# Four-layer graph kernel, layer 1: two adjacency gathers asked earlier, feature scaling one tile ahead instead of two, and SyncE's last adjacency tile ahead of a read-back

## The chip, the cores and the metric

One core of a Trainium2 chip runs the whole program. The metric is the device time of one execution in microseconds (us); the median of three executions stands for a kernel. Beside the times there is one profiled execution, with a trace of every instruction and every DMA packet.

## The reference

Four layers act on a graph of N = 2708 nodes with D = 128 features. `adj` (2708 x 2708, float32) is sparse, a fraction of a per cent of its entries, and has a filled diagonal. After each layer the input is added and the rows are normalised:

```python
x = _layernorm(x + L0(x, adj, adj, W0, a0))   # signed attention, dense product with adj
x = _layernorm(x + L1(x, adj, W1, b1))
x = _layernorm(x + L2(x, adj, W2, a2))        # four-head attention over the neighbours
x = _layernorm(x + L3(x, adj, ...))           # a gelu message for each neighbour, a gelu update, a layernorm

def L1(H, A, W, b):
    A_t = A + eye(n)
    D_inv = A_t.sum(axis=1) ** -0.5
    HW = H @ W.T + b
    return relu(D_inv[:, None] * A_t * D_inv[None, :] @ HW)
```

Layer 1 therefore needs the row sums of `adj` before it can scale the rows of HW by D_inv. The kernel takes these sums from lists of each row's nonzero entries, which it builds with a search, and which layers 2 and 3 use as well.

## The kernel before

**Tiles.** Rows are handled in NB = 22 blocks of 128. A product of a layer with `adj` runs on TensorE (PE) in two passes, each over a share of the output columns. In layer 0 pass 0 covers columns 0 to 1535, pass 1 the rest; in layer 1 pass 0 covers 0 to 2047 (four PSUM banks), pass 1 the remaining 660 (one bank of 512 and one of 148). Each pass goes over all 22 row blocks `n`; block `n` needs one adjacency tile `ah` and one block of features. Every product of a block with one bank shows as two matmuls in the trace.

**Adjacency tiles.** All 88 tiles (2 layers x 2 passes x 22) go through one pool of 7 buffers. `load_ahead(limit)` (line 846) asks for further tiles in this order, up to the limit and at most 7 beyond the tiles whose products have been written into the program (`done`). Layer 0 and layer 1's pass 1 fetch plain blocks with DMAs of SyncE (line 860; 330 KB for a tile of layer 1's pass 1). Layer 1's pass 0 works on rows in an order sorted by degree (`PERM`), so its tiles of 1 MB are indirect gathers, issued by GpSimd (POOL, line 853). In numbers of the pool, tiles 0 to 43 are layer 0's, 44 to 65 layer 1's pass 0, 66 to 87 its pass 1.

**Order.** `pinned` (line 265) chains the compute instructions and the GpSimd gathers of each engine in the order in which the program writes them. SyncE's plain loads are not pinned; the scheduler places them by their dependencies. Each engine executes its own list in order, and an instruction that waits holds everything behind it.

**Layer 0, pass 1.** `each0` (line 979) runs once per block: it takes signs on ScalarE (ACT), searches rows on VectorE (DVE) and, for the last blocks, prepares layer 1. `features(k)` (945) is a GpSimd gather of block k of the table TH, which the `finish` steps of layer 0 write to DRAM, into HS. It is called for k = 0 at n = 18, for k = 1 at n = 19, and for k = 2 and 3 at n = 21. `given(range(8))` (935) at n = 21 turns the search results of blocks 0 to 7 into DS, the factor D_inv in sorted order: one VectorE sum and three GpSimd operations.

**The search.** `entries` (614) goes over the blocks: it gathers a block's rows whole (`nat`, 1.4 MB, GpSimd line 621, four buffers), finds the largest entries with VectorE's MAX8 and their places with FIND_INDEX8 (about 3 us each). It runs through layer 0's passes and layer 1's pass 0. `given_back(b)` (595) writes block b's list to the DRAM table TL, in the natural order of rows; GpSimd issues it.

**Layer 1, pass 0.** `each1` (1053) at block n, after the products of block n: at n = 1 a small product and copy that adjust W2 (L1065, L1066), `features(n + 4)`, a stretch of search (at 1.35 units), `given` for the next two blocks at each even n, and `weights(n + 2)` (952), which scales HS block n + 2 in place by DS on ScalarE. Blocks 0 and 1 are scaled ahead of the pass by `scale_first` (955). After `each1` come `load_ahead(base + n + 6)` and two steps of each unfinished `finish` generator of layer 0. `finish` (748) takes a bank of results through a fixed sequence: transposes on PE, sums on VectorE (L769), means on GpSimd (L306, L307), squares on ScalarE (L312), roots on GpSimd (L316 to L318), normalisation on ScalarE (L322), transposes (L787), a copy `xt` (L790), a product with W1 (L824), an addition on VectorE (L827) and the write of TH. Three such banks are still open when layer 1 begins, so their steps lie between the products of blocks 0 to 4.

**Layer 1, pass 1.** `each1` with h = 1 calls `given_back(9 + n)` up to the last block at n = 12. At n = 13 (`NB - GIVEN`) it calls `natural_lists` (1018): SyncE reads TL back into LN when all the writes of TL have landed, and GpSimd copies three further columns. At n = 19 `off_diagonals` (1034) makes TOPJ on VectorE from LN (L1043 to L1048). In this pass the products of blocks 18 to 21 are done last, bank by bank: bank 4 of the four blocks, then bank 5, with their results copied out (L922) and put through `finish`, which writes TA to DRAM. Pass 0 ends with the products of block 21 alone, and between its banks with the step that brings D_inv back into the order of rows (L577).

**After it.** Layer 2 begins with 22 GpSimd gathers `ga` (L1183) of TA by TOPJ; layer 3 with gathers `G` (L1449) of the table TD, which layer 2 writes.

Of the kernel before, what the change touches and what calls it, by code (L numbers as in the profile page):

```python
# [118 lines left out]
def sparse_path(  # L119
# [28 lines left out]
    nc = tc.nc  # L148
    N, D = x.shape
    NB = -(-N // P)  # L150
# [114 lines left out]
    def pinned(i):  # L265

        e = i.ins.engine
        if e in newest:
            tc.add_manual_dep(
                i.ins, newest[e].name,  # L270
                mybir.DependencyInfo(mybir.DependencyClass.NoSync, mybir.DependencyReason.DATA),
                reason="order",
            )
        newest[e] = i.ins
        return i
# [102 lines left out]
    with (  # L378
# [16 lines left out]
        def features(bs):  # L395
            n = len(bs)
            g = slice(bs[0], bs[-1] + 1)
            xt = transposed([X[:, b, :] for b in bs], ps)
            t = ps.tile([P, 4, D], F32, name="hw_ps")
            for i, b in enumerate(bs):  # L400
                nc.tensor.matmul(t[:, i, :], xt[:, blk(i)], W0, start=True, stop=True)
            nc.scalar.copy(H[:, g, :], t[:, :n, :])
            for i, b in enumerate(bs):
                junk = sb.tile([P, D], F32, name="junk")
                nc.vector.scalar_tensor_tensor(
                    junk, t[:, i, :], 1.0, A1, ALU.mult, ALU.mult, accum_out=U[:, b : b + 1]
                )
            parts(UW[:, g, :], U[:, g], sb, n)
# [176 lines left out]
    GIVEN = 9  # L585
# [131 lines left out]
    with (  # L717
# [119 lines left out]

        loaded, done = [], [0]  # L840

        def span_of(layer, h):
            half = PASSES[layer][h]
# [2 lines left out]
        def load_ahead(limit=4 * NB):  # L846
            while len(loaded) < min(limit, 4 * NB, done[0] + BUFFERS):
                (layer, h), jb = divmod(len(loaded) // NB, 2), len(loaded) % NB
                lo, hi = span_of(layer, h)
                a = incoming.tile([P, EDGE], F32, name="ah")[:, : hi - lo]  # L850
                loaded.append(a)
                if layer and not h:
                    pinned(G_.indirect_dma_start(
                        a, None, adjL, bass.IndirectOffsetOnAxis(ap=PERM[:, jb : jb + 1], axis=0)
                    ))
                    continue
                for side, at in ((adjL, 0), (adjR, EDGE)):
                    k = slice(max(lo, at), min(hi, at + side.shape[1]))
                    if k.start < k.stop:
                        nc.sync.dma_start(  # L860
                            a[:, k.start - lo : k.stop - lo],
                            side[blk(jb), k.start - at : k.stop - at],
                        )
# [71 lines left out]
        def given(bs):  # L935

            while summed[0] <= bs[-1]:
                search(0.5)
            g = slice(bs[0], bs[-1] + 1)
            pinned(V_.tensor_reduce(SD[:, g], V[:, g, :], AX.X, ALU.add))  # L940
            pinned(G_.tensor_tensor(SD[:, g], SD[:, g], SELF[:, g], ALU.add))
            pinned(G_.tensor_scalar(SD[:, g], SD[:, g], 1.0, 1e-30, ALU.add, ALU.max))
            pinned(G_.tensor_tensor(DS[:, g], SD[:, g], HALF[:, : len(bs)], ALU.pow))
# [8 lines left out]
        def weights(k):  # L952
            pinned(S_.activation(HS[:, k, :], HS[:, k, :], AF.Copy, scale=DS[:, k : k + 1]))  # L953
# [11 lines left out]
        for h, half in enumerate(PASSES[0]):  # L965
            blocks = range(half[0] * 4, min(NB, half[-1] * 4 + 4))
            z = pz.tile([P, BANK], F32, name="z")[:, :48].rearrange("p (b k) -> p b k", k=4)
            behind = []

            def pattern(z=z, blocks=blocks, behind=behind):  # L970

                n, m = behind.pop()
                for i in range(len(blocks)):
                    pinned(T_.matmul(
                        z[:, i, :], m[:, blk(i)], F4[:, n, :],
                        start=n == 0 and i == 0, stop=n == NB - 1, skip_group_check=True,
                    ))

            def each0(n, a, lo, hi, h=h, behind=behind, pattern=pattern):
                if h == 0 and n + 2 < NB:  # L980
                    scaled(n + 2)
                m = signs[n % 2]
                if h and n < 2:
                    nc.gpsimd.memset(m[:, hi - lo :], 0.0)
                pinned(S_.activation(m[:, : hi - lo], a, AF.Sign))  # L985
                if behind:
                    pattern()
                behind.append((n, m))
                if h == 0 and n in (0, 3):
                    next(ordered, None)  # L990
                if h == 0 and n == 3:
                    next(passes)
                if h or n >= 8:
                    search(0.75 if h else 1.0)
                if h and NB - 4 <= n < NB - 2:
                    features(n - NB + 4)
                if h and n == NB - 1:
                    given(range(EARLY))
                    features(2)
                    features(3)  # L1000

            if h == 0:
                ordered = order(pt, nat)
                next(ordered)

            def end0(z=z, blocks=blocks, pattern=pattern):
                pattern()
                g = slice(blocks[0], blocks[-1] + 1)
                sums = RZ[:, g]
                nb = len(blocks)  # L1010
                pinned(S_.copy(zc[:, :nb, :], z[:, :nb, :]))
                pinned(V_.tensor_copy(CNT[:, g], zc[:, :nb, 3]))
                pinned(V_.tensor_reduce(sums, zc[:, :nb, 0:3], AX.X, ALU.add))
                pinned(V_.tensor_scalar(sums, sums, 1e-30, None, ALU.max))
                pinned(V_.reciprocal(sums, sums))

            later = half_of(0, h, H, each0, end0, later)
        def natural_lists():

            i = nc.sync.dma_start(  # L1020
                LN[:, :, : 2 * SLOTS], TL.rearrange("(b p) c -> p b c", p=P)
            )
            for name in back:
                tc.add_manual_dep(
                    i.ins, name,
                    mybir.DependencyInfo(mybir.DependencyClass.Sync, mybir.DependencyReason.DATA),
                    reason="all rows are in their places",
                )
            pinned(i)
            pinned(G_.tensor_copy(LN[:, :, K_ - 3], DEG))  # L1030
            pinned(G_.tensor_copy(LN[:, :, K_ - 2], DG))
            pinned(G_.tensor_copy(LN[:, :, K_ - 1], part["part"].to_broadcast([P, NB])))
# [18 lines left out]
        for h in range(2):  # L1051

            def each1(n, a, lo, hi, h=h):
                if h:
                    if GIVEN + n < NB:
                        given_back(GIVEN + n)
                    if n == NB - GIVEN:
                        natural_lists()
                    if n == 19:
                        off_diagonals()  # L1060
                    next(placed, None)
                    return
                if n == 1:
                    t = pt.tile([P, BANK], F32, name="q_ps")[:, : D + 2 * HEADS]
                    pinned(T_.matmul(t, C, W2, start=True, stop=True))  # L1065
                    pinned(S_.copy(W2, t))  # L1066
                if n + 4 < NB:
                    features(n + 4)
                search(1.35)
                k = n + 4  # L1070
                if EARLY <= k < NB and k % 2 == 0:
                    given(range(k, k + 2))
                if n + 2 < NB:
                    weights(n + 2)

            def end1():
                if later_half:
                    return
                for _ in passes:
                    pass  # L1080
                in_order_of_rows(pt, dinv, DS)
                for g in (slice(0, NB // 2), slice(NB // 2, NB)):
                    pinned(V_.tensor_tensor(
                        H2[:, g, :], H2[:, g, :],
                        dinv[:, g].unsqueeze(2).to_broadcast([P, NB // 2, D]), ALU.mult,
                    ))

            later_half = h
            later = half_of(1, h, H2 if h else HS, each1, end1, later)
# [83 lines left out]
    with (  # L1173
# [146 lines left out]
        last = len(sets) - 1  # L1320
# [11 lines left out]
        for t in ROWS:  # L1332
            n = NG - WHOLE
# [40 lines left out]
    with (  # L1374
# [256 lines left out]
        for n, k in enumerate(ORDER):  # L1631
# [7 lines left out]
            if n + 1 < NB:  # L1639
# [3 lines left out]
                i, j = place[k]  # L1643
# [542 lines left out]
```

## Time and profile before

| | |
|---|---|
| median of 3 runs | 650.23 us |
| lowest, highest run | 648.41, 655.59 us |
| profiled execution | 651.11 us, span of its instructions 649.3 us |
| busy share of the span | PE 73%, DVE 70%, POOL 57%, ACT 34% |
| mean granted clock of TensorE | 0.819 |
| data moved | 124.29 MB, mean 191 GB/s |
| layer 1, pass 0: first product to start of pass 1 | 176.5 to 280.4 us |
| layer 1, pass 1: to the last product's successor | 280.4 to 319.0 us |

Times inside the execution are counted from the first instruction of the span. "Idle before" is the time in which an engine did nothing ahead of an instruction, and the name behind it is what ended that wait. A gather's or load's landing is the time at which its completion was seen. Busy time is an average over stages with different limits, so the stage around an edit is read by itself: by the rows of each engine in order of time and by windows of a few microseconds.

### The profile page before, as it was taken

The page shows a single profiled execution, that of the slowest core. Times are in us where ns is not written, and L with a number is a line of the kernel's source. Part 1 is how long each engine was busy: PE and PEld are TensorE (multiplying, and loading weights), DVE is VectorE, ACT ScalarE, POOL GpSimd, SP SyncE. Part 2 cuts the span into 40 slices and gives each one's busy share as a digit, 9 for nine tenths or more (in the row PEclk, how much of TensorE's full clock was granted, in tenths as well). Part 3 has the DMA queues.
Part 4 walks back from the last instruction along what each step waited for, and adds up shares of the span by engine and source line. Part 5 has one row for each costly group of instructions (what it writes and reads, how often), then busy time and mean ns, then how long its engine had stood idle before and what let it go on. Part 6 is the DMA issues. An engine that isn't in the chain of part 4 may idle for free. (4 is left out here: it accounts for less than half of the span.)

```text
span 649.3 us, 8661 instructions
## 1 busy us (share of the span) xinstructions
PE 476.5 (73%) x2795; PEld 330.4 (51%) x2795; DVE 454.7 (70%) x1299; ACT 220.3 (34%) x519; POOL 372.8 (57%) x473
## 2 busy tenths in 40 slices
PE   6779999997856999899687565764765754665561
PEld 5644444664423443366386564553655643654560
DVE  3756999999995999462346838548638774584964
ACT  3125656685214000149543662221211211212120
POOL 6102023243474677537167657777777777777771
PEclk9559999999877999999855555987866869668687
DMA  9988999999599999957322121111212111121210
GB/s 305 380 318 311 406 424 405 395 344 393 195 379 362 334 411 417 362 180 212 97 73 49 52 77 48 45 48 44 63 44 63 46 50 47 45 59 48 56 43 26
DMA packets 46886, 124.29 MB, mean 191 GB/s; under 512 B 10303, under 2 KB 25077, under 8 KB 40559
## 3 DMA queue, kind: packets, MB, share of 16 engines
q0 software_dynamic: 15200, 69.06, 29.7%
q1 hardware_dynamic: 25230, 51.28, 22.1%
q10 hardware_dynamic: 6400, 3.30, 1.9%
q8 instruction: 24, 0.39, 0.2%
q14 instruction: 32, 0.25, 0.1%
HBM read 118.55 MB, written 6.30 MB: 192 GB/s over the span
## 5 line engine op out<-in xcount | busy, mean ns | idle before, releaser
L1449 POOL DMA_INDIRECT G<-TD,LP x126 | 131.3, 1042 | 44.8 <-issue 32.9
L878 PE MATMUL acc<-ah,XD 128*128 128x512 f32 (+1 forms) x264 | 114.1, 571 | 1.0 <-ACT XD L746 1.0
L1539 PE MATMUL af_ps<-W,M 128*128 128x128 f32 x426 | 77.3, 350 | 37.7 <-ACT M L1529 36.3
L655 DVE FIND_INDEX8 VI<-VI,nat 128x8 uint32<-128x2707 f32 x34 | 100.8, 2972 | 0.0
L1539 PEld LDWEIGHTS af_ps<-W,M 128*128 128x128 f32 x426 | 72.0, 260 | 41.2 <-ACT M L1529 39.6
L1449 POOL DMA_INDIRECT G<-TD,LM x63 | 63.6, 1010 | 19.2 <-issue 18.9
L985 ACT ACTIVATE sign<-ah 128x1536 bf16<-128x1536 f32 (+1 forms) x44 | 58.1, 1328 | 44.6 <-issue 26.3
L878 PE MATMUL acc<-ah,HS 128*128 128x512 f32 x132 | 64.7, 628 | 11.4 <-DMA ah<-in_adjL,PERM 6.7
L878 PEld LDWEIGHTS acc<-ah,XD 128*128 128x128 f32 x264 | 48.1, 197 | 44.8 <-issue 42.3
L1529 ACT ACTIVATE M<-M 128x1152 f32<-128x1152 f32 (+1 forms) x21 | 23.7, 1128 | 98.5 <-DVE M L1524 97.1
L1477 PE MATMUL q_ps<-S,JOIN 128*128 128x128 f32 x130 | 26.4, 354 | 35.5 <-DVE S L1473 35.5
L621 POOL DMA_INDIRECT nat<-in_adjo,PERM x22 | 21.9, 994 | 46.6 <-issue 19.8
L878 PEld LDWEIGHTS acc<-ah,HS 128*128 128x128 f32 x132 | 25.8, 202 | 42.5 <-issue 35.8
L1473 DVE TENSOR_TENSOR S<-sd_ps,MB 128x256 f32<-128x256 f32 x22 | 9.3, 421 | 51.4 <-PE sd_ps L1471 51.4
L1477 PEld LDWEIGHTS q_ps<-S,JOIN 128*128 128x128 f32 x130 | 21.2, 242 | 44.9 <-DVE S L1473 44.9
L642 DVE MAX8 cand<-nat 128x8 f32<-128x338 f32 (+3 forms) x96 | 34.8, 436 | 2.7 <-DMA nat<-in_adjo,PERM 2.7
L635 DVE MAX8 VI<-nat 128x8 f32<-128x2707 f32 x12 | 35.6, 2966 | 0.0
L1489 DVE TENSOR_SCALAR W<-TAB,LL 128x128 f32<-128x128 f32 x126 | 34.1, 358 | 0.0
L878 PE MATMUL acc<-ah,H 128*128 128x512 f32 (+1 forms) x88 | 28.3, 466 | 2.9 <-DMA ah<-in_adjR 2.9
L953 ACT ACTIVATE HS<-HS,DS 128x128 f32<-128x128 f32 x22 | 8.8, 400 | 62.8 <-DMA HS<-TH,PERMB 40.0
L1549 ACT COPY aT<-af_ps 128x128 f32<-128x128 f32 x22 | 5.8, 265 | 69.6 <-PE af_ps L1539 69.6
L1183 POOL DMA_INDIRECT ga<-TA,TOPJ x22 | 23.4, 1065 | 9.8 <-issue 9.8
(333 smaller groups left out, 951.7 us busy)
## 6 DMA issues: line engine op xcount, KB each, us to landing
ah<-in_adjL SPq DMA_DIRECT2D x22, 768.0 KB, 14.0
ah<-in_adjR SPq DMA_DIRECT2D x44, 330.0 KB, 7.3
TOP<-in_high SPq DMA_DIRECT2D x5, 1408.0 KB
ah<-in_adjL SPq DMA_DIRECT2D x22, 256.0 KB, 7.7
G<-TD,LP POOLq DMA_INDIRECT x126, 2.5
TA<-XD ACTq DMA_DIRECT2D x5, 264.0 KB, 3.6
TH<-H ACTq DMA_DIRECT2D x5, 256.0 KB
TD<-YD SPq DMA_DIRECT2D x3, 384.0 KB, 2.8
```

What stands on the lines that cost most here:

```text
L621: pinned(nc.gpsimd.indirect_dma_start(t, None, adjo, bass.IndirectOffsetOnAxis(ap=PERM[:, b : b + 1], axis=0)))
L635: pinned(nc.vector.max(V[:, b, 0:8], t))
L642: pinned(nc.vector.max(c[:, 8 * k : 8 * k + 8], t[:, at]))
L655: pinned(nc.vector.max_index(IX[:, b, s], V[:, b, s], t))
L878: pinned(T_.matmul(acc[i][:, :w], weights[:, n, :], a[:, i * BANK : i * BANK + w], start=n == 0, stop=n == NB - 1,))
L985: pinned(S_.activation(m[:, : hi - lo], a, AF.Sign))
L1183: pinned(G_.indirect_dma_start(ga[:, i, :], None, TA, bass.IndirectOffsetOnAxis(ap=TOPJ[:, b : b + 1], axis=0)))
L1449: i = G_.indirect_dma_start(G[:, s, :], None, TD, bass.IndirectOffsetOnAxis(ap=source(k, s), axis=0), **bound,)
L1477: pinned(T_.matmul(q[:, i, :], JOIN[:, j, :], S[:, :D], start=True, stop=True))
L1489: pinned(V_.tensor_scalar(W[:, s, :], part["lane"], to, v, ALU.is_equal, ALU.mult))
L1529: pinned(S_.activation(M[:, :n, :], M[:, :n, :], AF.Gelu))
L1539: i = T_.matmul(to, a, b, start=start, stop=stop, skip_group_check=True)
```

## The change

Six edits, none of which adds or takes away an operation. Two of them only serve the third part.

```diff
-        loaded, done = [], [0]
+        loaded, done, asked = [], [0], [None]
...
-                        nc.sync.dma_start(
+                        asked[0] = nc.sync.dma_start(
...
-                if h and NB - 4 <= n < NB - 2:
-                    features(n - NB + 4)
+                if h and n == NB - 4:
+                    features(0)
                 if h and n == NB - 1:
+                    load_ahead(2 * NB + 2)
                     given(range(EARLY))
+                    load_ahead(2 * NB + 3)
+                    features(1)
                     features(2)
                     features(3)
...
+            tc.add_manual_dep(
+                i.ins, asked[0].ins.name,
+                mybir.DependencyInfo(mybir.DependencyClass.NoSync, mybir.DependencyReason.DATA),
+                reason="the last tile is asked for first",
+            )
             pinned(i)
...
-                    if n == NB - GIVEN:
+                    if n == 17:
                         natural_lists()
...
-                if n + 2 < NB:
-                    weights(n + 2)
+                if 2 <= n + 1 < NB:
+                    weights(n + 1)
```

- **Early gathers.** At the end of layer 0's pass 1 (n = 21) the gathers of pool tiles 45 and 46 (blocks 1 and 2 of layer 1's pass 0) are written into GpSimd's list, one ahead of `given(range(8))` and one behind it. Before, they came with the products of layer 0's last bank, after `features(3)`. `features(1)` moves from n = 19 to behind them. Tile 44 was and is asked after n = 17.
- **Scaling.** `weights` for blocks 2 to 21 is called one block later, at n = k - 1 instead of n = k - 2.
- **SyncE.** `natural_lists` is called at n = 17, when the program has written all 88 loads, and its read-back of TL gets an order dependency (no wait of its own) on the last of them: SyncE must request the last tile of pass 1 before the read-back.

## Prediction

> **What bounds the kernel now.** I began with the chain of waits, because it says which stretch sets the end, and then walked back from its start. Merged by line it names GpSimd's gathers of layers 2 and 3, and its first piece stands at 323 us:
>
> ```profile
> POOL 23%; issue 11%; DMA 6%; DVE 5%; PE 3%; ACT 1%; POOLq 0%; DVEq 0%; ACTq 0%
> ```
>
> ```profile
> 323.24 0.78 ACT squares L312 x4
> ...
> 331.44 1.20 POOL ga L1183
> ```
>
> From 331.44 on (start and length in us) GpSimd issues 22 gathers `ga` and then the `G` gathers nearly without a break, to the end. Nothing there is edited. Those gathers need table TA, which the end of layer 1 writes. So whatever layer 1 saves before 323 moves the whole rest by the same amount, and what it loses too. Next I read layer 1's two passes on TensorE (start, length, what, idle before and its releaser):
>
> ```profile
> 176.46 2.84 PE L878 MATMUL acc<-ah,HS 128*128 128x512 f32 x6 [0.67 <-ACT HS L953]
> ...
> 187.10 5.46 PE L878 MATMUL acc<-ah,HS 128*128 128x512 f32 x6 [6.73 <-DMA ah<-in_adjL,PERM]
> ...
> 204.42 2.08 PE L824 MATMUL q_ps<-W,xt 128*128 128x128 f32 x8 [4.79 <-ACT xt L790]
> ...
> 262.37 2.84 PE L878 MATMUL acc<-ah,HS 128*128 128x512 f32 x6 [3.20 <-ACT HS L953]
> ...
> 315.33 3.81 PE L878 MATMUL acc<-ah,H 128*128 128x512 f32 x10 [2.91 <-DMA ah<-in_adjR]
> ```
>
> One tile of the gathered pass takes 3.43 us where nothing waits (216.75, 220.19, 223.62 and so on), 22 of them 75.5 us; from 176.46 to the pass's end at 280.4 there are 104. The missing 28 us lie mostly before tile 4 (212.88): tile 1 waits for its adjacency, tile 3 stands behind a wait for `xt`. What holds `xt` is in ScalarE's and VectorE's rows:
>
> ```profile
> 203.49 0.40 ACT L953 ACTIVATE HS<-HS,DS 128x128 f32<-128x128 f32 x1 [6.14 <-DMA HS<-TH,PERM]
> 203.80 0.56 ACT L790 COPY xt<-o_ps 128x512 f32<-128x512 f32 x1
> ```
>
> ```profile
> 206.53 0.69 DVE L827 TENSOR_TENSOR H<-q_ps,B 128x512 f32<-128x512 f32 x1 [7.78 <-PE q_ps L824]
> ```
>
> ScalarE stands in order: the scaling of tile 4's features, asked two tiles ahead, waits until 203.47 for a gather issued at 189.67, and the copy behind it, the two products behind that and VectorE's row search wait too. From 207 to 264.4 VectorE then searches almost without a gap, and its last result (DS) releases the last tile's gathers (266.09 and 267.47). So the 7.78 us come back at the pass's end. Last, the windows (stretch, length, busy times of PE, PEld, DVE, ACT, POOL, PE clock, DMA share, GB/s):
>
> ```profile
> 171.00:174.00 3.00, 3.00 (x12) 1.56 (x11) 2.94 (x13) 0.02 (x1) 2.50 (x5) 1.00 0.67 181
> 174.00:177.00 3.00, 2.16 (x14) 1.48 (x13) 2.83 (x13) 1.18 (x4) 2.50 (x3) 1.00 0.73 307
> 177.00:180.00 3.00, 3.00 (x9) 1.28 (x8) 3.00 (x11) 1.19 (x5) 2.27 (x5) 1.00 0.48 98
> 180.00:183.00 3.00, 0.38 (x3) 0.14 (x1) 3.00 (x11) 1.24 (x7) 2.16 (x3) 1.00 0.85 332
> ```
>
> The transfers rest for 0.99 + 0.81 + 1.56 + 0.45 = 3.8 us here, while six tiles are still unasked; from 183 to 207 the share is 0.97 to 1.05.
>
> **Part 1, gathers of tiles 1 and 2.** Nothing is added: GpSimd issues the same instructions in another order, so its own time (0.95 + 0.30 us per issue) stays. The place is behind features(0), which waits for TH until 169.16, so the hole from 165 to 169 stays open. From the rows of before the new order is: features(0) 169.16, `nat` 170.47, tile 1 at 171.7 (it was 180.23), the sums to 175.05, tile 2 at 175.2 (was 181.54), features(1), (2), (3) at 176.7, 177.9, 179.2 (were 171.73, 175.24, 176.65), `nat` 180.5 (was 177.96), then as before; from 185 on nothing on GpSimd has moved. features(1) now stands behind 2 MB. `nat` alone landed at 176.76; 1 MB behind another took 2.5 us (landings 191.95, 194.43). Tile 1 lands near 179.3, tile 2 near 181.8, features(1) just behind (it landed 0.2 us behind `nat` before). Its scaling (0.40) ends near 182.5, so tile 1 starts at 182.5 instead of 187.10. The moved `nat` lands near 186 instead of 184.43; VectorE needs it only after 201, so that costs nothing. Next comes a catch: before tile 2 TensorE has transposes (L787) of a block that ScalarE normalises (L322) after GpSimd's L318, at 192.18 and not moved. They began at 194.71 and can begin at 192.9. TensorE therefore idles from 186.3 to 192.9, and its clock falls as it did after 6.73 us (0.50 in the windows from 186 to 192). Tile 2 then runs some 2 us longer and ends near 199.5, where it ended before. So by itself this part brings almost nothing until tile 3.
>
> **Part 2, scaling one tile ahead.** 20 of the 22 scalings move one step later in ScalarE's order; none is added. At step 2 the scaling is now tile 3's, whose features land near 182, not tile 4's. `xt` is copied near 196 instead of 203.80; L824 runs when tile 2 ends (199.5 instead of 204.42), VectorE's L827 at about 200.6 instead of 206.53: 5.9 us. The second block's norm needs its L318 (198.87; up to 1 us earlier, as its squares are) and ends near 199.5, so tile 3 starts near 201.5 instead of 207.14: 5.6 us. TensorE has no idle of 4.79 us before it, so the slow clock from 204 to 210 (0.50, 0.58) goes as well, worth about 1.2 us more. What is late next: the transfers. From 213 to 273 they are full but for 0.2 us at 222 and 0.5 at 225, and `nat` lands 0.1 us ahead of its search (252.24 for 252.33). They can move by the holes that close: of 3.8 us about 2 (1.8 remain before tile 1 is moving and around 182), 0.9 at 210 to 213, 0.7 at 222 to 228: 3.6; counted by landings instead (1 MB at 215.10, 5.25 us behind the one before, could follow in 2.5) 2 + 2.7 + 0.7 = 5.4. Search, transfers and TensorE thus allow 5.9, 3.6 to 5.4 and 5.6 to 6.8. The least decides; I take 5.0 for the end of the pass, nearer to the count by landings, since a row shows each of those, with 3.6 and 5.9 as ends.
>
> **Part 3, SyncE's last tile.** SyncE held the read-back LN<-TL at the head from 302.2 until TL had landed (308.42), and with it the request for tile 21, whose buffer TensorE left at 304.65 (tile 14):
>
> ```profile
> 308.61 0.38 SPq L1020 DMA_DIRECT2D LN<-TL  x1
> 309.10 2.47 SPq L860 DMA_DIRECT2D ah<-in_adjR  x1
> ```
>
> Asked at 304.8, landing 3.6 us later (the median of these loads), it is there at 308.4, well before TensorE wants it at 312.42. The 2.91 us of idle go. The ten products behind it took 3.64 us at a clock of 0.56; at full clock, two 512-wide ones of 0.43 us and eight 148-wide ones of 0.13 (the tile at 303.54, two of each, took 1.11) would take 1.9. So TensorE's L755 moves from 318.97 to between 316.1 and 314.3. The read-back is asked at 308.6 as before (its request waits on TL, not on the tile) and takes 4.94 us at the most; VectorE's four instructions behind it end at 315.71 or up to 1.3 earlier. L761 was at 319.61, so 315.0 to 315.7 is possible: 3.9 to 4.6 us; 2.9 if the clock is no better. I take 4.0. The three copies of LN's columns that move with it on GpSimd (0.23 each) have 13.86 us of idle behind them. The Trainium skill, "TensorE: Matmul & The Clock Gate", section "Why this matters for your kernels", advises against TensorE idle gaps above about 3 us, after which the clock halves. A gap of 2.91 us is below that, so by the rule this part would keep its 2.9 us alone and the whole would be 642.3. The trace doesn't agree in either direction: 2.91 us before 315.33 was followed by 0.56, 3.20 us before 262.37 by 1.00.
>
> **Sum.** 5.0 + 4.0 = 9.0 us. The profiled execution took 651.11 (span 649.3 and 1.8 around it), giving 642.1; it lies 0.9 above the median of 650.23, so on that scale 641.2.
>
> **The rivals.** *Transfers alone bound the pass*, or the search starves on a later `nat`: then closing the first hole is undone by the full stretch from 213 to 273, and pass 0 ends 0 to 2 us earlier; only part 3 is left, 644.2 to 646.2. For it speak the share near 1.0 and the 0.1 us margin; against it the holes after 207, which come from the same stall. The Trainium skill, "DMA: Bandwidth & Descriptors", section "Issuing engines are not separate DMA queues", says that all issuers share the same 16 engines, so that an earlier request wins only idle time; the full shares agree. *Part 3 is refilled*: the read-back, not the tile, is late, or TL comes later, and VectorE's search for TOPJ ends last: only pass 0's 5.0 us count, 645.2. Against it: TOPJ is 3.9 us early now. *The early gathers don't go early*, should GpSimd's order leave them behind the features: then `xt` is still free, but the 2 us of the first hole stay open: 5.0 - 2 + 4.0 = 7.0, so 643.2. Against it: their buffers were last read before 164. *Slower:* a scaling one tile ahead is too late. TensorE then waits before each tile for ScalarE as it did at 255.47, for 0.78 us; 20 times that is 15.6, less the 9.0: 656.8. It decides from the point where the scaling leaves ScalarE less than 0.8 us before the product; the features of tiles 14 and 16 landed only 1.4 and 0.5 us ahead. Against it: from step 5 on ScalarE does nothing but scalings in this pass, so the order has no other work to put ahead, and each starts when its features land.
>
> **How the numbers follow.** Forecast case 0.58; transfers bound 0.18; part 3 refilled 0.10; gathers not early 0.06; slower 0.08. Under 1% (6.5 us, so 643.7) a measurement of this kernel can't be told from no change. The forecast case falls short of that with some 0.04, where its low ends meet; of the three middle cases, 0.34 together, 0.08 go below it: faster 0.62, same 0.30, slower 0.08. The range runs from 637.9 (5.9 and 4.6 saved, and 1.8 for the distance of the lowest run shown from the median) to 647.0 (the worst of the middle cases, 646.2, with 0.8); outside it lie the slower case and about a tenth of the rest.
>
> **What would show it.** Right: `ah` gathers at about 171.7 and 175.2; tile 1 at 182 to 183; no wait of 6 us for HS before `xt`; L824 near 200; the search's last instruction 3.6 to 5.9 us before 264.4; LN<-TL as SyncE's last request of the layer, TensorE without the idle of 2.91; the first `ga` near 322. Wrong: the pass ending after 278, many waits of ScalarE's HS at TensorE, or VectorE's L761 right behind L1048 with `ga` later than 326.

## The result, and the profile after

The changed kernel takes 642.57 us, the median of four runs (640.0 to 647.11), beside 650.82 us for the kernel before in the same runs (median of four): a ratio of 0.986, 95% interval 0.982 to 0.991, or 5.9 to 11.9 us less. The forecast was 641.2 us. The profiled execution is the longest of the four, 647.11 us with a span of 645.3, so single numbers from it are read by stage. Here and below, ratios, their intervals and differences of means leave out runs more than 1.5% above the fastest of their kernel, a slower state; medians are of all runs. In the changed kernel VectorE's instructions behind the read-back are L1051 to L1056 (L1043 to L1048 before), the first `ga` is L1191, the read-back L1023.

TensorE in order of time (start, length, what, count, idle before and its releaser); the columns are the same in all such lists below:

```profile
184.24 4.54 PE L878 MATMUL acc<-ah,HS 128*128 128x512 f32 x6 [3.71 <-ACT HS L953]
...
193.92 1.63 PE L787 MATMUL o_ps<-TAB,XD 128*128 128x128 f32 x4 [4.05 <-ACT XD L322]
...
257.08 4.24 PE L878 MATMUL acc<-ah,HS 128*128 128x512 f32 x6 [3.04 <-ACT HS L953]
...
314.27 1.32 PE L787 MATMUL o_ps<-TAB,XD 128*128 128x128 f32 x4 [2.91 <-DVE XD L769]
```

Tile 1 starts 2.9 us earlier than before, tile 2's transposes (L787) 0.8 us earlier. The wait of 4.79 us before L824 is gone, as this list from 199 us on shows:

```profile
200.35 1.05 PE L824 MATMUL q_ps<-W,xt 128*128 128x128 f32 x8
201.24 0.60 PE L787 MATMUL o_ps<-TAB,XD 128*128 128x128 f32 x4
201.68 2.74 PE L878 MATMUL acc<-ah,HS 128*128 128x512 f32 x6
```

ScalarE copies `xt` 7 us earlier (203.80 before), straight behind tile 3's scaling, with no wait:

```profile
196.47 0.39 ACT L953 ACTIVATE HS<-HS,DS 128x128 f32<-128x128 f32 x1
196.76 0.56 ACT L790 COPY xt<-o_ps 128x512 f32<-128x512 f32 x1
```

The windows that held the hole in the transfers (stretch, length, busy times of PE, PEld, DVE, ACT, POOL, PE clock, DMA share, GB/s):

```profile
171.00:174.00 3.00, 3.00 (x12) 1.52 (x11) 2.93 (x12) 0.00 (x0) 2.48 (x5) 1.00 0.43 83
174.00:177.00 3.00, 2.15 (x14) 1.61 (x13) 2.93 (x14) 1.17 (x3) 2.68 (x3) 1.00 0.93 385
177.00:180.00 3.00, 3.00 (x8) 1.28 (x7) 2.90 (x15) 0.00 (x0) 2.28 (x3) 1.00 1.00 411
180.00:183.00 3.00, 0.52 (x3) 0.14 (x1) 3.00 (x8) 0.00 (x0) 2.54 (x5) 1.00 0.88 358
```

From 174 to 180 the DMA engines rest for 0.2 us instead of 2.4, but from 171 to 174 for 1.7 instead of 1.0; over the four windows it is 2.3 us instead of 3.8. From 204 to 260 the transfers are as good as full. At the end of layer 1 SyncE asks for the read-back last, and VectorE is what the end then waits for. First SyncE, then VectorE:

```profile
290.00 11.43 SPq L860 DMA_DIRECT2D ah<-in_adjR  x7
305.77 0.38 SPq L1023 DMA_DIRECT2D LN<-TL  x1
```

```profile
311.08 0.43 DVE L1051 CAST LN<-LN 128x528 f32<-128x528 uint32 x1 [13.39 <-DMA LN<-TL]
311.55 0.71 DVE L1052 TENSOR_TENSOR nat<-LN,ROW 128x528 f32<-128x528 f32 x1
312.29 0.71 DVE L1055 TENSOR_TENSOR LN<-LN,nat 128x528 f32<-128x528 f32 x1
313.04 0.18 DVE L1056 CAST TOPJ<-LN 128x22 uint32<-128x22 f32 x1
313.13 0.87 DVE L761 SCALAR_TENSOR_TENSOR y<-H,o_ps 128x128 f32<-128x128 f32 x4
```

TensorE runs through its last tile without idle and has L755 out at 310.38, but L761 stands in VectorE's order behind four instructions that wait for the read-back until 311.08.

Four stamps say where the time went. P0 is from the first product of layer 1's first pass to the first of its second pass, P1 from there to the first L761 behind the last products (the row with x4), G from the first product to the first `ga`.

| kernel | P0 | P1 | G |
|---|---|---|---|
| before | 103.96 | 39.19 | 154.98 |
| changed | 99.93 | 36.60 | 148.71 |
| changed, two more profiles | 99.80, 99.44 | 35.22, 35.38 | 147.38, 147.66 |

So against this one profile of the kernel before, pass 0 gives 4.0 to 4.5 us, pass 1 2.6 to 4.0, and layer 1 as a whole up to the first `ga` 6.3 to 7.6.

### The profile page after: what moved, and what is told of

It is laid out like the page before. It is cut to its first block, busy times and chain, and to the rows that moved or that the text cites. A ratio compares the mean times of both kernels' runs of the same rounds, so it can differ in the third digit from the quotient of the medians.

```text
span 645.3 us, 8662 instructions
## 1 busy us (share of the span) xinstructions
PE 474.5 (74%) x2795; PEld 328.4 (51%) x2795; DVE 455.1 (71%) x1299; ACT 220.3 (34%) x519; POOL 374.2 (58%) x473
## 5 line engine op out<-in xcount | busy, mean ns | idle before, releaser
L1529 DVE TENSOR_TENSOR M<-G,q_ps 128x384 f32<-128x384 f32 x20 | 11.0, 548 | 27.5 <-DMA G<-TD,LM 27.4
L1191 POOL DMA_INDIRECT ga<-TA,TOPJ x22 | 24.4, 1110 | 10.1 <-issue 10.1
```

The costliest lines, as they stand in the source:

```text
L1191: pinned(G_.indirect_dma_start(ga[:, i, :], None, TA, bass.IndirectOffsetOnAxis(ap=TOPJ[:, b : b + 1], axis=0)))
```

## The experiments

Except for the last, these runs fell on chips where the kernel before itself takes about 696 to 703 us (medians of its runs), since the stretch behind the first `ga` takes 364 to 372 us there instead of 318 to 320. Differences of a few us can't be read from single whole times there, so the stamps are read.

**One part at a time.** Early gathers alone, scaling alone, SyncE's part alone, and the first two without the third; each is the kernel before with these edits of the diff:

```diff
# early gathers alone
+                if h and n == NB - 4:
+                    features(0)
...
+                    load_ahead(2 * NB + 2)
                     given(range(EARLY))
+                    load_ahead(2 * NB + 3)
+                    features(1)
# scaling alone
+                if 2 <= n + 1 < NB:
+                    weights(n + 1)
# SyncE's part alone
+                i.ins, asked[0].ins.name,
...
+                    if n == 17:
                         natural_lists()
```

Early gathers alone:

> Only the early gathers of tiles 1 and 2 and the later features(1) are kept; scaling and SyncE as before. Theory: scaling and gathers are worth something only together, since tile 2 of pass 0 stands behind a norm that GpSimd's list releases, and xt behind the scaling of tile 4. So tile 1 starts near 184 instead of 187.1, but L824 still waits for xt until about 203 and pass 1 starts at 278.5 to 280.4 (before 280.42, after 276.53). Rival, the gathers alone carry the gain because the transfers bound the pass: pass 1 starts at 276 to 277.5. LN<-TL and the last tile as before: TensorE idle of 2.9 us before the last products.

Scaling alone:

> Only the scaling one tile ahead is kept; gathers and SyncE as before. Theory: xt no longer stands behind the scaling of tile 4, so VectorE's L827 comes near 200.5 instead of 206.5 although tile 1 still starts at 187; the hole of the transfers from 171 to 183 stays, so pass 1 starts at 277.5 to 279 (2 to 3 us of the 3.9). Rival, the scaling matters only when the gathers are early, or costs waits at each tile: pass 1 starts at 280 or later, with more than five waits of TensorE for the scaled features from tile 5 on.

SyncE's part alone:

> Only SyncE's part is kept: the last tile of pass 1 ahead of the read-back. Theory: pass 0 as before (pass 1 starts at 280.4), TensorE loses its idle of 2.9 us and the slow clock behind it, so that L755 comes 4.7 us earlier (from 38.6 us after the start of pass 1 to 33.9), but the read-back lands about 1 us later and VectorE's L761 stands behind the four instructions on it: L761 comes only 2.5 to 2.7 us earlier (36.6 us after the start of pass 1 instead of 39.2), and so does the first ga. Rival, the read-back is no wait of its own and L761 follows L755: 4.6 us earlier.

The first two without the third:

> Gathers and scaling are kept, SyncE's part is undone. Theory: pass 1 starts near 276.5 as in the changed kernel, TensorE idles 2.9 us before the last products, L761 is 39.2 us after the start of pass 1, the first ga near 327.5 to 328 (before 331.44, after 325.31). Rival, the gain of pass 0 is eaten before ga without SyncE's part: first ga after 330.

| kernel | P0 | P1 | G | one time |
|---|---|---|---|---|
| gathers alone | 103.00 | 36.83 | 152.07 | 698.56 |
| scaling alone | 99.90 | 39.01 | 151.17 | 701.25 |
| SyncE's part alone | 106.75 | 36.49 | 155.69 | 705.59 |
| gathers and scaling | 99.37 | 39.53 | 150.86 | 692.87 |

By P0 the scaling alone gives all of pass 0's gain (more than the 2 to 3 us expected of it), the gathers alone 1 us. But SyncE's part has the instructions of before in pass 0 and yet a P0 of 106.75, so a difference of less than 3 us in one profile's P0 isn't a result by itself. Where that scatter comes from can be read at tile 17, the last tile before which TensorE waits for long in these kernels. From the start of tile 17 to the start of pass 1 it takes 18.0 to 18.1 us at full clock and more behind a half clock:

| kernel | first product to tile 17 | tile 17 to pass 1 |
|---|---|---|
| before | 85.91 | 18.05 |
| gathers alone | 83.25 | 19.75 |
| scaling alone | 81.81 | 18.09 |
| SyncE's part alone | 85.81 | 20.94 |
| gathers and scaling | 81.32 | 18.05 |
| changed, three profiles | 80.48, 80.05, 81.40 | 19.45, 19.75, 18.04 |

With SyncE's part alone tile 17 starts where it did before, at 262.37, and its products then run at half clock, 5.49 us instead of 2.84:

```profile
262.37 5.49 PE L878 MATMUL acc<-ah,HS 128*128 128x512 f32 x6 [3.04 <-DMA ah<-in_adjL,PERM]
```

So up to tile 17 the gathers alone bring 2.7 us, the scaling alone 4.1, both 4.5 to 5.9 in four profiles; the half clock behind the wait of about 3 us then costs 0 to 2.9. What the gathers add to the scaling, 0.4 to 1.8 us, is of the size in which profiles of one kernel differ (1.35 us).

In P1 the parts do not mix: 36.49 with SyncE's part alone, as in the changed kernel, 39.0 to 39.5 without it. One exception shows the cost of the slow clock: with the gathers alone TensorE's idle before the last tile was 2.23 us instead of 2.91, the granted clock stayed at 1.00, and P1 was 36.83 without any edit there. Beside that profile SyncE's part is worth 1.6 us at most; the rest of its gain is the slow clock, and 0.6 to 1.2 us more of idle, that the other three profiles without it had there.

**Same kernel again, lists behind the row sums, no early gathers, 2 MB more.** These four shared a chip. The second writes VectorE's four instructions behind layer 1's last row sums; the third does the same and takes the early gathers out.

```diff
# lists behind the row sums
-                    if n == 19:
-                        off_diagonals()
...
         for _ in placed:
             pass
+        off_diagonals()
# 2 MB more
+                if n in (9, 11):
+                    pinned(G_.dma_start(SCR[: 128, :], adjL[: 128, :]))
```

> The changed kernel as it is, on the same chip as the next three. Stage times, from its profile: layer 1's second pass starts 99.4 to 100.4 us after the first product of its first pass; L761 of the last bank stands 36.6 us behind that start, some 2.1 to 2.8 us behind the L755 that feeds it; the first ga is 148.5 to 149.5 us behind the first product. Ratio to the kernel before 0.982 to 0.991.

Measured: P0 99.80, P1 35.22, G 147.38; ratio 0.987, interval 0.982 to 0.991 (twelve runs, median 692.38, beside 702.26). P1 came out 1.4 us better than expected, since the read-back was asked 0.56 us earlier after the start of pass 1 and landed 4.50 us after its request instead of 5.31.

> Theory: what the third part gives back is VectorE's order. Its four instructions behind the read-back (2.1 us, and a wait for the read-back ahead of them) stand ahead of layer 1's last row sums (L761), which need no list. With the four behind the last row sums, L761 follows its L755 by about 0.65 us, stands 34.5 us behind the second pass's start instead of 36.6, and the first ga comes 2.1 us earlier against the first product than in the changed kernel; the whole is 2 us (0.3%) below the changed kernel, since the gathers ga of table TA need the table and TOPJ, and TOPJ ends no later than now. Rival: the read-back itself is what the end waits for, since ga needs TOPJ; then ga does not move (under 0.5 us), and only L761 does.

Measured: P1 34.50 and L761 0.64 us behind its L755, as the theory has it. The order on VectorE is shown by this list:

```profile
313.50 0.88 DVE L761 SCALAR_TENSOR_TENSOR y<-H,o_ps 128x128 f32<-128x128 f32 x4 [13.48 <-PE o_ps L755]
...
316.80 0.42 DVE L1051 CAST LN<-LN 128x528 f32<-128x528 uint32 x1
...
318.74 0.18 DVE L1056 CAST TOPJ<-LN 128x22 uint32<-128x22 f32 x1
```

The first `ga` stood 46.72 us behind the start of pass 1, beside 48.78, 47.58 and 48.22 in the three profiles of the changed kernel: 0.9 to 2.1 us earlier. The rival fell: `ga` moved with L761, though TOPJ ended later. The whole time doesn't show it: median 693.92 of six runs, ratio 0.988 (0.980 to 0.996), and P0 was 103.13 with the same instructions in that pass. Why is in GpSimd's list and the windows of this kernel:

```profile
220.15 0.94 POOL L853 DMA_INDIRECT ah<-in_adjL,PERM  x1 [0.31 <-issue]
230.69 0.95 POOL L948 DMA_INDIRECT HS<-TH,PERMB  x1 [9.60 <-DMA TH<-H]
```

```profile
224.00:228.00 4.00, 4.00 (x11) 1.85 (x10) 4.00 (x2) 0.31 (x1) 0.00 (x0) 1.00 0.95 391
228.00:232.00 4.00, 3.42 (x8) 1.16 (x7) 4.00 (x4) 0.00 (x0) 1.21 (x3) 1.00 0.08 31
```

The first gather of features from TH's second half (tile 12's) waits for the last write of TH. That write was issued at 210.36 and its last packet ended at 229.58: 19 us for 128 KB beside full queues of gathers. GpSimd stood, and the transfers ran dry for some 5 us. In the changed kernel the write was issued at 213.24, landed 9.50 us later and the gather at 224.28 found it done, with 1.5 us to spare. This is a wait that the prediction didn't see.

> Scaling one tile ahead, SyncE's order and the lists behind the row sums, but the gathers of tiles 1 and 2 where they were. Theory: the scaling alone gives the whole of the first pass (99.9 us between the starts of the two passes with it alone, 99.4 to 99.9 with both), so this kernel takes the same time as the one with the lists behind the row sums, within 1 us, though tile 1 starts 2 us later. Rival: the early gathers close a hole in transfers that are the bound afterwards, so without them the first pass is 2 to 3.7 us longer, and the whole 0.3 to 0.6% slower.

Measured: P0 99.33, P1 34.34, G 145.85, the shortest G of all kernels that compute everything; but the profiled execution (692.86 us) is the second shortest of the twelve runs. The whole says otherwise: median 696.7 of twelve runs, ratio 0.995 (0.990 to 1.000), beside 692.4 for the changed kernel and 693.9 for the one with the lists behind the row sums on the same chip. Its mean is 4.5 +/- 2.9 us above the first of these and 3.2 +/- 3.3 above the second. The stage of one profile is for the theory, the whole speaks for the rival; where the time goes stays open. Both kernels with the new scaling and without early gathers had GpSimd waiting for the last write of TH (3.18 and 3.71 us), but so had the one with the lists and the early gathers (9.60), so this wait doesn't decide it.

> The changed kernel with two copies of 1 MB from table to scratch memory, which nobody reads, issued by GpSimd at tiles 9 and 11 of layer 1's first pass. Theory: from 204 us on that pass is bound by its transfers (share of the 16 engines about 1.0), so 2 MB more, at 2.5 us per MB read, lengthen it by about 5 us (99.9 to about 105 between the starts of the passes), with the new waits on TensorE between tiles 10 and 18. Rival: VectorE's row search or TensorE bounds it and the transfers have room; then it is 0 to 1.5 us longer.

Measured: P0 104.38, 4.6 us longer; tile 17 starts 86.3 us behind the first product instead of 80.1 to 81.4. VectorE and TensorE (one list each) wait where they had not, or longer:

```profile
252.40 2.98 DVE L635 MAX8 VI<-nat 128x8 f32<-128x2707 f32 x1 [5.26 <-DMA nat<-in_adjo,PERM]
```

```profile
244.27 2.84 PE L878 MATMUL acc<-ah,HS 128*128 128x512 f32 x6 [3.81 <-ACT HS L953]
...
255.59 4.54 PE L878 MATMUL acc<-ah,HS 128*128 128x512 f32 x6 [4.19 <-ACT HS L953]
```

Even the search waits for its rows now, 5.26 us, where its longest wait in the three profiles of the changed kernel was 0.74. GpSimd needed 0.6 us for each of the two copies, so issuing them isn't the cost. That is what the theory says.

**Fewer bytes, and both early gathers first.** One kernel gathers and multiplies 64 rows instead of 128 in tiles 8 to 15; one is the changed kernel again; the third puts both early gathers ahead of `features(0)`, with the lists behind the row sums.

```diff
# 64 rows in tiles 8 to 15
+                    some = slice(0, P // 2 if 8 <= jb < 16 else P)
...
+                        a[some, :], None, adjL,
# both early gathers first
                 if h and n == NB - 4:
+                    load_ahead(2 * NB + 3)
                     features(0)
```

> The changed kernel, but the eight tiles 8 to 15 of layer 1's first pass gather and multiply 64 of their 128 rows: 4 MB less to transfer, the same number of instructions, and a product that leaves half the rows of these tiles out. Theory: transfers set the end of that pass once the scaling is free. Then tile 17's adjacency and features land some 8 to 10 us earlier, TensorE's waits before tiles 14 to 17 (5 to 6 us together) and the slow clock behind the longest of them (1.4 us) go, and the next limit, the last tiles' gathers behind VectorE's search, leaves 94 to 97 us between the starts of the two passes instead of 99.8. Rival: VectorE's search sets the end, being as good as without a gap from 201 to 260; then the waits move but the passes' starts stay 99 to 100 us apart. The search's own end should move by less than 1 us in either case.

Measured: P0 103.15, and the question not answered. TensorE's waits before tiles 14 to 17 went from 3.1 to 6.2 us together (three profiles of the changed kernel) to one of 2.15, none before tile 17, as the theory asks; but in its windows TensorE's clock (third column from the end) stands at 0.50 from 239.0 to 259.5:

```profile
225.00:239.00 14.00, 13.16 (x31) 5.42 (x29) 13.96 (x10) 0.80 (x2) 11.29 (x17) 1.00 1.04 259
239.00:254.00 15.00, 13.69 (x16) 5.16 (x16) 13.86 (x8) 1.30 (x4) 10.88 (x19) 0.50 1.00 384
254.00:259.50 5.50, 5.50 (x7) 2.18 (x7) 3.93 (x7) 0.70 (x2) 2.71 (x6) 0.50 1.01 408
```

Half the rows also did not halve the transfers' time: the share stayed at 1.04 while only 259 GB/s moved.

> The changed kernel as it is, for the ratio of the next kernel. 99.4 to 103 us between the starts of layer 1's two passes (two kernels with the same instructions in that pass gave 99.8 and 103.1), L761 35.2 to 36.6 behind the second start, ratio to the kernel before 0.982 to 0.991.

Measured: P0 99.44, P1 35.38, G 147.66, first `ga` at 322.67; ratio 0.993 (0.990 to 0.997) on this chip, above the 0.982 to 0.991 expected; medians 695.91 and 702.68.

> The lists behind the row sums, and the gathers of tiles 1 and 2 both ahead of the features of tile 0, which hold GpSimd until table TH is written (about 169.5 us): they go out near 165 and fill the hole in the transfers from 165 to 171. Theory (transfers set the pass's end): tile 1 starts 2 to 3 us earlier, at its features' scaling; the two gathers land by 172, the later transfers move 2 us ahead, and the first pass is 1 to 3 us shorter than the changed kernel's 99.8, the first ga 2 to 4 us earlier, the whole about 0.4% below the changed kernel. Rival: the wait moves to the writes of TH, which stand behind full queues of gathers (9.5 us in the changed kernel's profile, and 19 us for the kernel with the lists behind the row sums, where GpSimd stood 9.6 us before tile 12's features and the transfers ran dry): then the first pass is no shorter, 99.5 to 103.

Measured: P0 99.92, P1 34.46, G 146.85; ratio 0.993 (0.989 to 0.997), no better than the changed kernel beside it. The rival was right about the stage, with another write than it named. GpSimd's list and the windows of this kernel:

```profile
172.80 0.95 POOL L948 DMA_INDIRECT HS<-TH,PERM  x1 [15.09 <-DMA TH<-H]
```

```profile
171.00:174.00 3.00, 2.83 (x14) 1.65 (x13) 3.00 (x14) 0.58 (x1) 1.14 (x2) 1.00 0.05 15
174.00:177.00 3.00, 0.62 (x6) 0.39 (x4) 2.83 (x16) 0.28 (x1) 2.70 (x4) 1.00 0.49 123
```

The first part of TH now lands behind the two gathers, so `features(0)` goes out 2.6 us later than in the changed kernel (170.20), and the hole in the transfers has only moved from before 171 to behind it.

**Four tiles multiplied twice.** The question that the 64 rows left open, without the slow clock:

```diff
+                if layer and not h and jb in (9, 11, 13, 15):
+                    loaded.append(loaded[-1])
+                    continue
```

> The changed kernel, but tiles 9, 11, 13 and 15 of layer 1's first pass gather no adjacency and multiply the rows of the tile before them a second time: 4 MB less to transfer (10 us at 2.5 us per MB), all products with their full 128 rows; the sums of these four tiles are left out. It asks again what the kernel with 64 rows could not answer, since TensorE's granted clock stood at 0.50 for 20.5 us while it multiplied 64 rows. Theory (transfers set the pass's end): no wait over 1 us before tiles 14 to 17, the clock stays at 1.00 from 200 to the end of the pass, and 94 to 97 us lie between the starts of the two passes; the last wait is then before one of the last three tiles, whose gathers stand behind VectorE's search. Rival (VectorE's search sets the end): 99 to 100 us.

Measured, on a chip where the kernel before takes 653.19 us: P0 95.17, P1 35.46, 639.6 us in all. Two windows of it:

```profile
220.00:230.00 10.00, 10.00 (x25) 4.47 (x24) 10.00 (x8) 1.10 (x3) 6.26 (x9) 1.00 0.72 265
...
250.00:260.00 10.00, 8.49 (x19) 3.07 (x17) 8.95 (x5) 1.21 (x3) 6.16 (x12) 1.00 0.99 373
```

The transfers have room (0.72), the granted clock stays at 1.00, no wait before tiles 14 to 17 is over 0.8 us, and pass 0 is 4.8 us shorter, while the search ends 82.4 us behind the first product, as in the changed kernel (82.7). GpSimd also issues four gathers fewer, but its list was not full: in the changed kernel it waits 5.4 us for VectorE between 210 and 260. So in the changed kernel transfers set the end of pass 0 and the search does not; the rival fell.

## Why the prediction was right, and where its terms were off

**Nothing past 323 us.** The stretch behind the first `ga` was 317.9 us in the profile before, 320.0 in the longest run of the changed kernel. The time by medians (8.3 us) lies somewhat above what layer 1 gave in three profiles (6.3 to 7.6), inside the interval of 5.9 to 11.9. That the time came within 1.4 us of the forecast is in part luck: layer 1 gave 6.3 us in the profile shown where 9.0 were forecast, and both terms of the sum came out low there.

**Part 1.** The hole in the transfers closed by 1.5 us, for the forecast 2. The order on GpSimd was as read: `ah` at 172.77 and 176.28 for the forecast 171.7 and 175.2, the difference being `features(0)`, released 1.04 us later by TH. Tile 1 started at 184.24 instead of 182.5: features(1) was scaled at 183.78, right behind the second gather's landing at 183.49, which had been put at 181.8. The catch before tile 2 was there (4.05 us of idle, L787 at 193.92 for 192.9), and "by itself almost nothing" held at the pass's end: 1 us alone, after 2.7 at tile 17. The price in the rival about the gathers is not borne out by the stage: without them 2 us less were to be had, and P0 with the scaling alone was the same (99.90 and 99.33). The whole times lean to such a price (4.5 and 3.2 us, with wide intervals); that is the open question above.

**Part 2.** `xt`, L824 and L827 came at 196.76, 200.35 and 201.44, for 196, 200 and 200.6; the search's last instruction ended 5.1 us earlier. Transfers as the next limit is shown from both sides, with 2 MB more and 4 MB less. The end of pass 0 moved by 4.0 us and not 5.0, inside the ends of 3.6 and 5.9. At the start of tile 17 it was 5.4 us; the missing part is in the row at 257.08: six matmuls in 4.24 us, at half clock behind 3.04 us of idle, where before the same place had 3.20 us of idle and the clock stayed. The same wait of 3.04 us in the kernel with the two first parts cost no clock, and its P0 is 99.37 though its tile 17 starts 0.8 us later. The prediction carried over the clock of before, which was chance.

**Part 3.** It was the term that was over-sized in the profile shown: 2.6 us for the forecast 4.0. TensorE's side was right and at its best end: no idle, L755 33.85 us behind the pass's start. The step that failed is "the read-back is asked at 308.6 as before and takes 4.94 us at the most". Against the start of pass 1 it was asked 1.05 us later (TL's last write took 4.75 us to land instead of 3.85) and took 5.31, without any load beside it. VectorE's four instructions then ended 36.69 us behind the pass's start instead of 35.29, and L761 behind them. This is the rival "refilled" in part: VectorE's TOPJ ends last in every kernel with SyncE's part and the old order on VectorE, where 1.5 to 2.8 us lie between L755 and L761 instead of 0.64. In the two other profiles of the changed kernel the read-back took 4.5 and 4.6 us and P1 was 35.2 and 35.4, so 3.8 to 4.0 us were gained there. The forecast's baseline was a matter of luck too: the slow clock of before was counted as a fixed part of what there was to gain, and the kernel with the gathers alone shows a P1 of 36.83 without it.

**The clock rule.** The prediction found 2.91 us of idle followed by 0.50 and 3.20 us followed by 1.00 and left it there. All 82 stretches of the granted clock that begin between 165 and 310 us, in fourteen traces, are multiples of 3.413 us long. Cut into such pieces, the idles differ. The 2.91 us before 315.33 lay whole in one piece (311.9 to 315.3, 85% of it), and the next was granted half. Before, around 262, the idle of 3.20 us falls half into one piece and half into the next:

```profile
257.30:260.70 3.40, 1.87 (x5) 0.56 (x3) 3.40 (x2) 0.00 (x0) 2.93 (x4) 1.00 1.01 408
260.70:264.10 3.40, 1.73 (x4) 0.87 (x5) 3.37 (x3) 0.40 (x1) 1.14 (x2) 1.00 1.01 410
```

In the changed kernel most of a shorter idle falls into one piece, and the next one is granted half:

```profile
253.10:256.50 3.40, 0.94 (x3) 0.11 (x1) 3.37 (x4) 0.00 (x0) 2.69 (x4) 1.00 1.03 415
256.50:259.90 3.40, 2.81 (x4) 1.27 (x5) 2.86 (x2) 0.40 (x1) 0.88 (x4) 0.50 1.02 410
```

The Trainium skill, "TensorE: Matmul & The Clock Gate", section "Part 1: The HAM clock gate (the "warmup" mystery)", says that the gate looks at TensorE's activity in free-running windows of 3413 ns; these traces agree (3.413 us). That would have been the page to weigh here, not the rule of about 3 us.

**The other rivals.** No scaling was late: TensorE waited for HS before three tiles late in the pass, 5.1 us together; before the longest, tile 17's features had landed at 256.61, 0.5 us ahead of the product. The slower case did not come.

## What to carry to other kernels

When a stall in an in-order engine goes, ask which queue is next and test it from both sides, with bytes added and bytes taken away; one side alone would have left VectorE's nearly gapless search as an explanation. When a load is moved ahead of a read-back, look at what stands behind the read-back on the engine that uses it: here four instructions without haste stood in front of the path, and writing them behind it brought 0.9 to 2.1 us of the stage. When two profiles differ by a few us, look first at whether an idle cost the clock: the same instructions gave 103.96 and 106.75 us here. A saving in one stage that moves small writes or gathers into full queues is worth what those writes let through, so read their landings too.

## What the runs showed of the hardware

- Between 175 and 309 us of thirteen traces, 31 pieces of 3.413 us at full clock were followed by half clock, and TensorE idled for 58 to 100% of each; 421 were followed by full clock, with 0 to 59% idle. So the clock halved behind every piece with more than 60% idle and behind none with less than 57%. An idle of 2.50 us cost the clock in one kernel, one of 3.81 us cost none in another.
- With products over 64 rows half clock was granted behind a piece with only 0.87 us of idle (25%), and stayed for six pieces (20.5 us), although TensorE was busy for 13.7 of the first 15 us. That kernel isn't among the thirteen traces above. That the rows are the cause wasn't shown by a kernel of its own.
- In the stretch with gathers of 64 rows of 8 KB the engines moved 259 GB/s at a share of 1.04; with 128 rows it was 406 to 423 GB/s at 1.01 to 1.02 (the changed kernel from 210 to 260 us).
- A write of 128 KB in pieces of 512 bytes took 9.5 us to land in one profile beside full queues of gathers (the changed kernel) and 19 us in another (lists behind the row sums).
- On the chips with the longer times ScalarE's copy `aT` in layer 3 waited 12 to 15 times for something that the profile doesn't show, 104 to 128 us in all and up to 16.7 us at once (eleven traces); in the three traces with the shorter times these waits are not there. What it is was not tried.
